# Four cross-attention key projections moved into the first batch of a recurrence, and output projections one step later

## The chip, the cores and the metric

The kernel runs on one core of a Trainium2 chip. The metric is the device time of one execution in microseconds; smaller is better. The engines are TensorE (PE; its weight loads are shown as PEld), VectorE (DVE), ScalarE (ACT), GpSimd (POOL) and SyncE (SP), whose queue starts nearly all transfers here. Each engine takes its own instructions strictly in order; semaphores tie the engines together.

## The reference

Four layers in sequence, on x (8 x 256 x 512) and a context of the same shape, all float32. L0 is an attention with an injected context. L1 is a recurrence with channel mixing, L2 a decoder block (self-attention, cross-attention, MLP), L3 a product with the context. The part that matters:

```python
# L1: for each batch, along 256 positions
a = k_l[..., :, None] * v_l[..., None, :]
out = jnp.einsum('bhs,bhst->bht', r_l, faaaa * a + s)
s_new = a + w_l[..., None] * s
...
# L2, D = 512, 16 heads of 32
ctx = merge_heads(attention(split_heads(q), split_heads(k), split_heads(v), ltor_mask))
x = hidden_states + (ctx @ w_ao + b_ao)
q = layernorm(x, ln2_s, ln2_b) @ w_q + b_q
kv = encoder_states @ w_kv + b_kv
k, v = jnp.split(kv, 2, axis=-1)
ctx = merge_heads(attention(split_heads(q), split_heads(k), split_heads(v), cross_mask))
x = x + (ctx @ w_co + b_co)
```

The keys and values of the cross-attention depend on the context input and on weights only, not on what the layers before have computed.

## The kernel before, in words

The program has three stages. `stage_l0` computes L0. `Middle` computes L1 and both attentions of L2 in one loop. `stage_mlp` does the rest. The change lies in `Middle`, whose code is in `plan`.

**The recurrence.** Its loop has 64 steps: 8 batches x 4 column tiles `ct` x 2 halves. In a step `spread` (L890, PE) writes products into the one PSUM buffer `vb`; `states` multiplies them with k (L912) and scans them (L916, two scans, DVE); POOL multiplies by r (L921); `gather` (L933, PE) sums the step before. A spread can start only when the scans of the step before have read `vb`.

**The attentions.** 16 runs of 4 steps follow: runs 0 to 7 (`a_`) are the self-attention of the batches 0 to 7, runs 8 to 15 (`c_`) the cross-attention. A step handles 4 heads of 32. In step n the loop issues the row maxima (L1121, DVE) and exponentials (L1124, ACT) of step n+1, the transpose `dt` of half of step n's probabilities (L1157, DVE, which goes through DRAM to `pt`), the scores of step n+2 (L1102, PE) with their masking (L1111 product on DVE, L1116 addition on POOL), the other half's transposes (L1146, PE), the reciprocals and divisions of step n+1 (L1132 DVE, L1134 POOL), and `values` of step n-1 (L1174, PE, copied to `cx` by ACT at L1178).

**Fillers.** All other work hangs in these loops by a `Filler`: a table from a slot number to functions. `fill.until(x)` runs all that is due up to x. In the recurrence, step n first runs `states`, then fillers up to n + 0.95, then `gather`, then fillers up to n + 0.99, then the next `spread`. In the attention a step runs its fillers up to n + 0.5 before `values` and up to n + 0.99 after it; A0 = 64 is where the attention's slots begin, and run i has its slots at A0 + 4i plus a number. So the projections of q, k and v of a run (`at_q`, `at_k`, `at_v`) lie in the steps of the run before, and its output projection (`at_out`, two halves) in the steps of the run after: half 0 at 4.6, that is after `values` of step 0 of the next run, half 1 at 5.6, after `values` of step 1. `proj` (L805) and `proj_s` (L869) are the matmuls of all of these. `at_out` adds the result to the residual tile `hv` or `csx` (L1068, DVE), `at_v` adds the bias to `av` (L1053, DVE).

**Order on the engines.** In `Middle` PE follows the program's order. On the other engines a scheduler orders by its own estimate of when an instruction's inputs are ready, except where an instruction is pinned behind the one traced before it on its engine (`pin`, that is `keep_in_program_order`). The masking, the maxima, the reciprocals, the divisions and `dt` are pinned; L1053 and L1068 are not.

**Buffers.** Weights are loaded by SP into a pool of ten halves (five pairs); a list `spans` of first and last use, sorted, decides at which slot each pair is loaded. The tags `kk` and `csx` have one buffer each, `k` has two, and the PSUM banks `mm` are three in the recurrence and eight in the attention.

Of the kernel before, what the change touches and what calls it, by code (L numbers as in the profile page):

```python
# [10 lines left out]
F32 = mybir.dt.float32  # L11
AF = mybir.ActivationFunctionType
ALU = mybir.AluOpType
# [3 lines left out]
P = 128  # L17
B, S, D = 8, 256, 512
ST = S // P
CT = D // P  # L20
# [73 lines left out]
def rows_of(halves):  # L94

    return [halves[k // 2][:, k % 2, :] for k in range(CT)]
# [513 lines left out]
class Middle:  # L610
# [62 lines left out]
    def plan(self):  # L673
        g, cp, wpool = self.g, self.cp, self.wpool
        nc, I = g.nc, g.I
# [32 lines left out]
        t_ = {}  # L708
# [91 lines left out]
        def proj(b, W, src, c2):  # L800
            pp = mm("proj")
            for j in range(2):
                o = (2 * c2 + j) * P
                for k in range(CT):
                    nc.tensor.matmul(  # L805
                        pp[:, j, :], lhsT=t_[W, b][k][:, o : o + P], rhs=src[:, k, :],
                        start=(k == 0), stop=(k == CT - 1),
                    )
            return pp
# [56 lines left out]
        def proj_s(b, W, src, st):  # L866
            pp = flat(mm("projs"))
            for k in range(CT):
                nc.tensor.matmul(  # L869
                    pp, lhsT=src[:, k, st * P : (st + 1) * P], rhs=t_[W, b][k],  # L870
                    start=(k == 0), stop=(k == CT - 1),
                )
            return pp
# [116 lines left out]
        HD, NH = 32, 4  # L990
        runs = [(pre, b) for pre in ("a_", "c_") for b in range(B)]

        def at_fetch(i):
            pre, b = runs[i]
            x = t_["axi", i] = wk.tile([P, ST, D], F32, tag="xi", name="axi", bufs=1)
            nc.sync.dma_start(out=x, in_={"a_": g.x2, "c_": g.x3, "m_": g.x4}[pre][b])
# [40 lines left out]
        def at_k(i, c2):  # L1037
            pre, b = runs[i]
            if c2 == 0:
                t_["ak", i] = wk.tile([P, CT, S], F32, tag="k", name="ak")  # L1040
            pp = proj(0, pre + "wk", t_["src", i], c2)
            for j in range(2):
                ct = 2 * c2 + j
                nc.scalar.activation(
                    t_["ak", i][:, ct, :], pp[:, j, :], AF.Identity, bias=g.pv(pre + "bk", ct)
                )

        def at_v(i, st):
            pre, b = runs[i]
            if st == 0:  # L1050
                t_["av", i] = wk.tile([P, ST, D], F32, tag="v", name="av")
            vp = proj_s(0, pre + "wv", t_["src", i], st)
            nc.vector.tensor_tensor(t_["av", i][:, st, :], vp, g.rv[pre + "bv"], ALU.add)  # L1053

        def at_residual(i):
            pre, b = runs[i]
# [7 lines left out]
        def at_out(i, st):  # L1064
            pre, b = runs[i]
            x = t_["axo", i]
            op = proj_s(0, pre + "wo", t_["cx", i], st)
            nc.vector.tensor_tensor(x[:, st, :], x[:, st, :], op, ALU.add)  # L1068

        def at_store(i):  # L1070
            pre, b = runs[i]
# [4 lines left out]
        def at_load(W, src, col):  # L1076
            t_[W, 0] = rows_of(g.weight(wpool, I[src], col, W))
# [10 lines left out]
        def at_consts2():  # L1088
            late = cp.tile([P, NMC], F32, tag="constc", name="lconstc")
            nc.scalar.dma_start(out=late[:, 0 : NRV - 2 * D], in_=I["rvec"][2 * D :].partition_broadcast(P))  # L1090
            for name, n in RVEC[2:]:
                c = RCOL[name] - 2 * D
                g.rv[name] = late[:, c : c + n]

        pin = lambda ins: self.tc.keep_in_program_order(ins)

        def scores(i, ct):
            sps = t_["sp", i, ct] = [mm("sp") for _ in range(NH)]
# [103 lines left out]
        def when(b, at):  # L1202

            if b == 0 and at in FIRST:
                return FIRST.index(at) - 30
            return 8 * (b - 1) + (at[max(0, b - B + 3)] if isinstance(at, tuple) else at)
# [3 lines left out]
        fill = self.fill = Filler()  # L1210
        for b in range(B):
            for at, fn, *args in steps + after:
                fill.put(when(b, at), lambda b=b, fn=fn, args=args: fn(b, *args))

        A0 = 8 * B
        for i in range(len(runs)):
            for at, fn, *args in (
                (-7.1, at_fetch), (-5.95, at_inputs), (-6.6, at_norm), (-5.9, at_normed), (-5.3, at_norm_T),
                (-4.8, at_q, 0), (-3.8, at_q, 1), (-2.8, at_k, 0), (-2.3, at_k, 1), (-1.3, at_v, 0), (-0.8, at_v, 1),
                (3.9, at_residual), (4.6, at_out, 0), (5.6, at_out, 1), (6.3, at_store),  # L1220
            ):
                fill.put(A0 + CT * i + at, lambda i=i, fn=fn, args=args: fn(i, *args))
        runs.append(("m_", 0))
        for at, fn in ((-6.1, at_fetch), (-5.6, at_norm), (-4.9, at_normed), (-4.3, at_norm_T)):
            fill.put(A0 + CT * (2 * B) + at, lambda fn=fn: fn(2 * B))
# [8 lines left out]
        spans = []  # L1234
# [3 lines left out]
        for pre, i, q, kv, o in (("a_", 0, "w_qkv", "w_qkv", "w_ao"), ("c_", B, "w_q", "w_kv", "w_co")):  # L1238
            c = D if q == kv else 0
            for W, lo, hi, src, col in (  # L1240
                ("wq", -4.8, -3.8, q, 0), ("wk", -2.8, -2.3, kv, c), ("wv", -1.3, -0.8, kv, c + D), ("wo", 4.6, 5.6, o, 0)
            ):
                lo, hi = A0 + CT * i + lo, A0 + CT * (i + B - 1) + hi
                spans.append((lo, hi, lambda W=pre + W, src=src, col=col: at_load(W, src, col)))
        spans.sort(key=lambda x: x[0])

        free = [-9.0, -9.0, -2.9, -0.9, 2.3]
        for lo, hi, fn in spans:
            free.sort()
            at = free.pop(0)  # L1250
# [507 lines left out]
```

## Time and profile before

| | us |
|---|---|
| three runs | 3474.51, 3485.38, 3486.36; median 3485.38 |
| profiled execution | 3492.2, its span 3490.3, mean granted clock 0.968 |
| recurrence's first spread | at 1394 |
| first transpose `dt` of the attention | at 2213 |
| last one | at 2972 |
| busy PE / DVE / ACT / POOL | 3262.3 / 2373.8 / 1606.1 / 1943.9 |
| a 512 KB load of a weight, of `enc`, of `xi`, issue to landing | 4.1 to 4.8, 4.5, 3.4 |

All stretches are counted from the start of the span. A line of instructions in order of time gives the start, the time from the first start to the last end, the engine, the line of code, the operation, the tiles, the count, and in brackets the idle time before it with what ended it. A line of waits gives who waited for whom, the total, how often, and the longest. The granted clock is TensorE's, as a share of its full speed.

### The profile page before, as it was taken

The numbers are of one execution on the slowest core, as the hardware profiler recorded it, in microseconds if no ns is written. First come the engines' busy times: TensorE is split into PE (matmuls) and PEld (weight loads), VectorE is DVE, ScalarE is ACT, GpSimd is POOL, SyncE is SP. The second block draws the span as 40 slices with busy tenths as digits, with TensorE's granted clock in tenths as the row PEclk, the third lists the DMA queues.
The fourth block names the chain that finished last, engine by engine and source line by source line (L and its number), as shares of the span: only waits on it lengthen the run. The fifth ranks groups of instructions, "written<-read, shape, count | busy, mean of one in ns | idle before, by whom it ended". The sixth has DMA issues, their size and how long they took to land. (4 is left out here: it accounts for less than half of the span.)

```text
span 3490.3 us, 68550 instructions
## 1 busy us (share of the span) xinstructions
PE 3262.3 (93%) x27008; PEld 2333.4 (67%) x27008; DVE 2373.8 (68%) x3328; ACT 1606.1 (46%) x4032; POOL 1943.9 (56%) x1870
## 2 busy tenths in 40 slices
PE   8999999999999998789999998799999998799999
PEld 6677776777777765566566665555565554699996
DVE  4666666666666663888887877565677766577771
ACT  3455555555555463233334333455656655323223
POOL 7533333333324222565565665667778888688882
PEclk9999999999999998899999999899999999899999
DMA  7666665665756533212233232244355445300002
GB/s 273 228 191 195 185 200 172 196 205 177 219 180 204 176 94 124 74 55 97 91 98 105 95 116 78 88 146 155 118 169 161 147 139 163 130 1 1 1 11 87
DMA packets 230431, 466.46 MB, mean 134 GB/s; under 512 B 19872, under 2 KB 114720, under 8 KB 226016
## 3 DMA queue, kind: packets, MB, share of 16 engines
q1 hardware_dynamic: 227648, 456.47, 40.8%
q8 instruction: 215, 3.52, 0.4%
q10 hardware_dynamic: 1808, 3.80, 0.3%
q0 software_dynamic: 656, 1.81, 0.2%
q14 instruction: 104, 0.85, 0.1%
HBM read 378.12 MB, written 83.89 MB: 132 GB/s over the span
## 5 line engine op out<-in xcount | busy, mean ns | idle before, releaser
L381 POOL TENSOR_SCALAR pe<-pe,rinv 128x512 f32<-128x512 f32 x256 | 177.8, 695 | 613.5 <-DVE rinv L380 608.3
L921 POOL TENSOR_TENSOR rs<-a,r 128x1024 f32<-128x1024 f32 x128 | 303.6, 2387 | 262.0 <-DVE a L916 259.2
L358 DVE TENSOR_REDUCE nmax<-sp 128x2 f32<-128x1024 f32 x256 | 309.0, 1218 | 185.3 <-PE sp L353 185.3
L367 ACT ACTIVATE pe<-sp,nmax 128x512 f32<-128x512 f32 x512 | 347.5, 683 | 11.4 <-ACT nmax L363 0.4
L1124 ACT ACTIVATE pe<-pe,nmax 128x256 f32<-128x256 f32 x512 | 253.3, 499 | 207.1 <-DVE nmax L1121 207.1
L393 DVE STREAM_TRANSPOSE pt<-pe 128x1024 f32<-128x1024 f32 x256 | 313.0, 1232 | 52.3 <-POOL pe L381 43.4
L422 PE MATMUL av<-pt,vr 32*64 32x256 f32 x8192 | 276.2, 397 | 38.7 <-issue 25.6
L916 DVE TENSOR_TENSOR_SCAN a<-w,vb 128x1024 f32<-128x1024 f32 x128 | 287.3, 2275 | 4.9
L422 PEld LDWEIGHTS av<-pt,vr 32*64 32x64 f32 x8192 | 213.1, 139 | 113.3 <-issue 45.7
L353 PE MATMUL sp<-k,q 64*64 64x512 f32 x2048 | 265.8, 611 | 8.2 <-ACT pe L367 8.2
L1134 POOL TENSOR_SCALAR pe<-pe,rinv 128x256 f32<-128x256 f32 x512 | 242.5, 496 | 3.1 <-DVE rinv L1132 2.3
L363 ACT ACTIVATE nmax<-nmax 128x2 f32<-128x2 f32 x256 | 51.8, 203 | 405.0 <-DVE nmax L358 404.6
L293 PEld LDWEIGHTS gp<-t,ws 128*128 128x128 f32 x1512 | 184.3, 192 | 32.0 <-issue 13.7
L1116 POOL TENSOR_TENSOR pe<-pe,lconstb 128x1024 f32<-128x1024 f32 x64 | 150.8, 2359 | 96.9 <-DVE rinv L1132 85.4
L293 PE MATMUL gp<-t,ws 128*128 128x128 f32 x1512 | 202.8, 278 | 1.9 <-POOL ws L279 1.4
L386 ACT ACTIVATE pe<-pe,rinv 128x512 f32<-128x512 f32 x256 | 182.5, 729 | 41.4 <-DVE rinv L380 41.4
L1121 DVE TENSOR_REDUCE nmax<-pe 128x4 f32<-128x1024 f32 x128 | 153.1, 1213 | 53.7 <-POOL pe L1116 53.7
L1116 POOL TENSOR_TENSOR pe<-pe,mb 128x1024 f32<-128x1024 f32 x64 | 151.1, 2361 | 66.9 <-DVE rinv L1132 65.9
L912 DVE TENSOR_TENSOR vb<-vb,k 128x1020 f32<-128x1020 f32 x128 | 157.2, 1228 | 4.4
L890 PE MATMUL vb<-v,mconstc 32*128 32x255 f32 x1024 | 99.8, 446 | 57.5 <-DVE a L916 57.5
L1438 ACT ACTIVATE h<-h,pvec 128x256 f32<-128x256 f32 x124 | 55.8, 500 | 200.7 <-DVE h L1407 163.2
L380 DVE RECIPROCAL rinv<-ssum 128x2 f32<-128x2 f32 x256 | 41.1, 161 | 147.0 <-ACT pe L367 147.0
(312 smaller groups left out, 7805.5 us busy)
## 6 DMA issues: line engine op xcount, KB each, us to landing
ws<-sqk SPq DMA_DIRECT2D x110, 512.0 KB, 5.0
wqk<-in_wqk_dram SPq DMA_DIRECT2D x71, 512.0 KB, 5.1
vr<-v SPq DMA_DIRECT2D x128, 256.0 KB, 4.8
pt<-dt SPq DMA_DIRECT2D x64, 512.0 KB, 2.6
pt<-pt SPq DMA_DIRECT2D x256, 128.0 KB, 3.1
ws<-sv SPq DMA_DIRECT2D x56, 512.0 KB, 5.0
wv<-in_wv_dram SPq DMA_DIRECT2D x36, 512.0 KB, 4.7
v<-vT SPq DMA_DIRECT2D x64, 256.0 KB, 2.6
```

Source lines behind the costliest of these rows:

```text
L293: nc.tensor.matmul(out[:, hf * P : (hf + 1) * P], lhsT=w[n](hf, k), rhs=a[n](hf, k), start=k == 0, stop=k == ST - 1,)
L353: nc.tensor.matmul(sp[a * 64 : (a + 1) * 64, h, :], lhsT=qs[b, 2 * un + a][r, ic], rhs=ks[b, 2 * un + a][r, :], start=True, stop=True,)
L358: nc.vector.tensor_reduce(nmax, sp, AX.X, ALU.max, negate=True)
L367: nc.scalar.activation(pe[:, h, :], sp[:, h, :], AF.Exp, bias=nmax[:, h : h + 1], scale=1.0 / DH ** 0.5, accum_out=ssum[:, h : h + 1],)
L386: nc.scalar.mul(pe[:, 1, :], pe[:, 1, :], rinv[:, 1:2])
L393: nc.vector.transpose(pts[b, un][:, it], pe)
L422: nc.tensor.matmul(av[r][h * DH : (h + 1) * DH], lhsT=vr[rows_, kb, h * DH : (h + 1) * DH], rhs=pt[rows_, :, h, 32 * kb : 32 * kb + 32], s ...
L916: nc.vector.tensor_tensor_scan(a.rearrange("p n l -> p (n l)"), w4.rearrange("p n l -> p (n l)"), vb[:, 4 * n2 : 4 * n2 + 4, :].rearrange( ...
L921: nc.gpsimd.tensor_tensor(rs, a, rb, ALU.mult)
L1116: pin(nc.gpsimd.tensor_tensor(pe4, pe4, b4, ALU.add))
L1124: nc.scalar.activation(pe[:, r, :], pe[:, r, :], AF.Exp, bias=nmax[:, r : r + 1], accum_out=ssum[:, r : r + 1],)
L1134: pin(nc.gpsimd.tensor_scalar(pe[:, r, :], pe[:, r, :], rinv[:, r : r + 1], 1.0, ALU.mult, ALU.mult))
```

## The change

It has three parts.

1. A key projection of the cross-attention, for batches 0 to 3 (runs 8 to 11), is computed in the first eight steps of the recurrence (`EARLY`), each from its own load of the context into `kk`, with a weight pair of its own (`c_wk0`). The result goes to `csx`, and from there to DRAM (`ck`). In the attention `at_k` loads it from DRAM into the tile `ak` in place of the projection. Runs 12 to 15 stay as they were.
2. The additions L1053 (`at_v`) and L1068 (`at_out`) are pinned.
3. The first half of the output projection goes from slot 4.6 to 5.2: from the end of step 0 to the middle of step 1, before `values`. The time at which its weights are expected moves with it.

```diff
+        pin = lambda ins: self.tc.keep_in_program_order(ins)
...
+            if pre == "c_" and b in ck:
+                if c2 == 0:
+                    nc.sync.dma_start(out=t_["ak", i], in_=ck[b])
+                return
...
+        EARLY = {0: (-0.3, 0.6, 1.6), 1: (1.7, 2.6, 3.2), 2: (3.25, 3.8, 4.6), 3: (4.7, 7.3, 7.7)}
+        ck = {}
+
+        def ck_load(b):
+            t_["enc", b] = wk.tile([P, CT, S], F32, tag="kk", name="enc", bufs=1)
+            nc.sync.dma_start(out=t_["enc", b], in_=I["ctxT"][b].rearrange("(k p) s -> p k s", p=P))
+
+        def ck_part(b, c2):
+            if c2 == 0:
+                t_["ck", b] = new("csx", 1)
+            pp = proj(0, "c_wk0", t_["enc", b], c2)
+            for j in range(2):
+                ct = 2 * c2 + j
+                nc.scalar.activation(t_["ck", b][:, ct, :], pp[:, j, :], AF.Identity, bias=g.pv("c_bk", ct))
+            if c2 == 1:
+                ck[b] = g.dram([P, CT, S], f"ck{b}")
+                nc.sync.dma_start(out=ck[b], in_=t_.pop(("ck", b)))
...
-            nc.vector.tensor_tensor(t_["av", i][:, st, :], vp, g.rv[pre + "bv"], ALU.add)
+            pin(nc.vector.tensor_tensor(t_["av", i][:, st, :], vp, g.rv[pre + "bv"], ALU.add))
...
-            nc.vector.tensor_tensor(x[:, st, :], x[:, st, :], op, ALU.add)
+            pin(nc.vector.tensor_tensor(x[:, st, :], x[:, st, :], op, ALU.add))
...
+        for b, (lo, *at) in EARLY.items():
+            fill.put(lo, lambda b=b: ck_load(b))
+            for c2 in range(2):
+                fill.put(at[c2], lambda b=b, c2=c2: ck_part(b, c2))
...
-                (3.9, at_residual), (4.6, at_out, 0), (5.6, at_out, 1), (6.3, at_store),
+                (3.9, at_residual), (5.2, at_out, 0), (5.6, at_out, 1), (6.3, at_store),
...
-                ("wq", -4.8, -3.8, q, 0), ("wk", -2.8, -2.3, kv, c), ("wv", -1.3, -0.8, kv, c + D), ("wo", 4.6, 5.6, o, 0)
+                ("wq", -4.8, -3.8, q, 0), ("wk", -2.8, -2.3, kv, c), ("wv", -1.3, -0.8, kv, c + D), ("wo", 5.2, 5.6, o, 0)
...
+        spans.append((0.55, 7.75, lambda: at_load("c_wk0", "w_kv", 0)))
```

More of the change, by code (lines that the diff above doesn't have):

```diff
@@ L1093, in at_consts2 @@
                 g.rv[name] = late[:, c : c + n]
-        pin = lambda ins: self.tc.keep_in_program_order(ins)
         def scores(i, ct):
```

## The prediction

> **What bounds the kernel now.** I read the page's busy shares first, then stretches of the span, the waits of the attention, and last the single instructions of each engine in order of time.
>
> ```profile
> PE 3262.3 (93%) x27008; PEld 2333.4 (67%) x27008; DVE 2373.8 (68%) x3328; ACT 1606.1 (46%) x4032; POOL 1943.9 (56%) x1870
> ```
>
> TensorE looks like the limit. By stretch (us of window, then busy PE, PEld, DVE, ACT, POOL, the clock, DMA share, GB/s) it is not so simple: 1399 to 1447 is the beginning of the recurrence, 2720 to 2765 is attention run 10.
>
> ```profile
> 1399.00:1447.00 48.00, 35.86 (x246) 24.20 (x245) 44.85 (x49) 5.11 (x10) 30.15 (x14) 0.82 0.11 34
> 2346.00:2391.00 45.00, 45.00 (x256) 27.32 (x255) 25.86 (x37) 23.60 (x77) 27.60 (x32) 1.00 0.47 153
> 2720.40:2764.90 44.50, 41.95 (x266) 26.71 (x265) 31.84 (x50) 27.53 (x89) 36.79 (x43) 1.00 0.47 151
> 2809.40:2855.40 46.00, 43.23 (x265) 27.58 (x264) 31.87 (x51) 27.88 (x91) 36.77 (x44) 0.96 0.44 144
> ```
>
> Early in the recurrence VectorE is the full engine (44.85 of 48) and PE has holes, at a low clock. Runs 0 to 3 of the attention still carry the recurrence's leftover matmuls: PE is 45.00 of 45 there. From run 4 on, PE is idle some 2.5 us a run. The waits of 2446 to 2945 name it (total, times, longest):
>
> ```profile
> DVE csx L1068 <- PE projs L869: 39.9, 12, 5.6
> PE projs L869 <- ACT cx L1178: 25.7, 10, 2.6
> ```
>
> The first output projection of a run waits for the last context tile, and VectorE waits for that projection before the next row maxima. What these waits cost is read from the cycle that carries a step. VectorE's transpose `dt` comes once a step, the mask addition on GpSimd follows:
>
> ```profile
> 2709.11 1.25 DVE L1157 STREAM_TRANSPOSE dt<-pe 128x1024 f32<-128x1024 f32 x1 [0.60 <-POOL pe L1134]
> 2710.28 1.25 DVE L1111 TENSOR_TENSOR pe<-sp,mk 128x512 f32<-128x512 f32 x2
> ...
> 2720.39 1.25 DVE L1157 STREAM_TRANSPOSE dt<-pe 128x1024 f32<-128x1024 f32 x1 [0.61 <-POOL pe L1134]
> ...
> 2728.85 0.69 DVE L1068 TENSOR_TENSOR csx<-csx,projs 128x512 f32<-128x512 f32 x1 [2.56 <-PE projs L869]
> 2729.46 2.34 DVE L1121 TENSOR_REDUCE nmax<-pe 128x4 f32<-128x1024 f32 x2
> 2731.71 1.24 DVE L1157 STREAM_TRANSPOSE dt<-pe 128x1024 f32<-128x1024 f32 x1
> ```
>
> `dt` waits for GpSimd's last division of the step before; GpSimd's next step waits for the mask product behind `dt`. GpSimd's step is 2 x 2.36 + 2 x 1.85 = 8.42 us (L1116, L1134), `dt` and the mask product 2 x 1.17, hand-overs some 0.2: 10.95. Measured starts of `dt` in run 9 are 2675.9, 2687.2, 2698.1, 2709.1, 2720.4: steps of 11.33, 10.93, 10.99, 11.28. So this GpSimd-VectorE cycle, at 10.92 to 10.95 us, sets the step; the wait of 2.56 us at L1068 cost 0.39 of it, GpSimd's residual additions 0.33. PE only has to keep up. Runs 4 to 13 last 47.21, 46.14, 44.45, 45.88, 45.92, 44.53, 44.53, 44.52, 45.92, 45.92 us (455.02); run 14 lasts 43.70. The longer ones have a lower clock (0.93 and 0.96 above), and PE limits some of their steps (12.28, 12.23 us).
>
> **Part 1: four key projections go into batch 0's recurrence.** Added there: four times two halves of 16 PE records. One half measures 3.55 us start to start at full clock, so 8 x 3.55 = 28.4 us of PE work, 16 evictions on ScalarE (0.42 each, ScalarE is 5.11 busy of 48), and on SP's queue one more weight pair, four loads of `enc`, four stores of `ck`. The cover is PE's idle time:
>
> ```profile
> 1434.61 2.08 PE L890 MATMUL vb<-v,mconstc 32*128 32x255 f32 x16 [6.28 <-DVE a L916]
> 1436.62 5.03 PE L805 MATMUL proj<-x_maa_k,Wk 128*128 128x256 f32 x16
> ...
> 1482.68 2.08 PE L890 MATMUL vb<-v,mconstc 32*128 32x255 f32 x16 [7.71 <-DVE a L916]
> ```
>
> Gaps of 4.32, 1.54, 6.28 and 7.71 us before spreads 1, 2, 4 and 8 make 19.85. After a gap PE runs slow: the spread takes 2.08 instead of 1.07, Wk 5.03 instead of 3.55. With the gaps filled that excess goes too; over 1404 to 1447 I count some 6 us of it. So 28.4 - 25.9 = 2.5 us at least.
>
> By place: batch 0's first half fits into the 4.32. The second half stands before the gather and the `mp` matmuls of step 1, delaying the next vb copy 0.5 us. Batch 1's first half lies between Wg and hp: delay 1.9 in all. In step 3 the new order has 7.1 us of PE before the gather, and they cannot run through: batch 2's `enc` shares one buffer with batch 1's and is issued only when that batch's last half is done (about 1431.9 by my count); a 512 KB load lands after 3.4 us at the quickest of the like rows (xi 3.4, enc 4.5), so PE stands some 3.9 us, and `mp` and spread 4 end near 1442 instead of 1436.7: 5.7. One more half in step 4 makes 7.2 to 7.6; steps 5 and 6 are limited by PE (13.00 of 13, 14.97 of 15 busy), so nothing is won back there; batch 3's 7.1 us fit the 7.71, and the warm spread returns 1.0. Sum **+6.6**. Bounds: 2.5 (all cover used) and 21.3 (nothing usable but the last gap, 28.4 - 7.1). I take 6.6 because each place was walked through.
>
> The gate: idle 6.28 us was followed by matmuls at 5.03/3.55 of their warm time, but idle 2.59 us was too (run 4's next two projection records: 2.08 against 1.13), in 4 of 10 cases. The Trainium skill, "TensorE: Matmul & The Clock Gate", Part 1, says the clock drops after an idle window of about 3.4 us. By that rule gaps of 2 us would never be slow, and the ordinary runs below would gain 5 us where I put 2; it also speaks against taking matmuls out of the attention, since that opens longer gaps.
>
> SP: what queues behind the new waits (Wr's second half, Wg of batch 1) is needed from step 6.3 and 8.5 on, 50 us later: nothing.
>
> **Part 2: what leaves the attention.** Keys of runs 8 to 11 were projected in the steps of runs 7 to 10: 7.1 us of PE each, and 4 evictions each. But those steps follow the GpSimd cycle. With 7.1 us of slack PE no longer limits any, and the L1068 wait goes: 10.94 + 10.94 + 10.99 + 11.27 = 44.14 a run, 176.6 against 45.88 + 45.92 + 44.53 + 44.53 = 180.9: **-4.3**. The `ck` loads (512 KB) are queued one run early, since their buffer is free then; the transposes' own transfers (2.6 and 3.1 us) have a whole step: nothing, and at most 3 us each if they collide.
>
> **Part 3: first output projection to the next step, additions pinned.** In the order of instructions only L1068 moves: before, the first addition stood ahead of the row maxima of the next step; now both stand together, one step's end later. The `av` additions (L1053) stay where they were, except one near the recurrence's end that no longer sits between two scans (0.66 us, **-0.6**).
>
> Step 0 of a run loses its 0.39. Step 1, however, now has on PE: transposes 0.95, projection 3.5, keys 3.55, values 1.0, projection 3.5, keys 3.55, scores 1.1. Its transposes wait for GpSimd's division, 4.2 us before `dt`. So the second projection ends 8.3 us after `dt`; add hand-over 0.2, one addition 0.65, two maxima 2.35: the next `dt` at 11.6 instead of 10.94, **+0.7**. PE also idles in step 0, in two pieces (1.7 and 2.1 us) where it had one of 2.6. Run: 10.95 + 11.65 + 10.99 + 11.27 = 44.86 if warm. The six ordinary runs (4, 5, 6, 11, 12, 13) took 274.2; six times 44.86 is 269.2, so -5.0 if none is slow, and +1.0 if four lose 1.5 as four did. I take the middle, **-2.0**: the gaps are shorter, but there are two. Run 14, at 43.70: **+0.7**. Runs 0 to 3 are full of PE work whose amount stays: 0 (bounds -6, the idle between 2212 and 2335 that nothing here touches, and +3 x 2.9 if step 1 turns slow).
>
> Sum: 6.6 - 4.3 - 2.0 + 0.7 - 0.6 = +0.4 us. The profiled execution took 3492.2 (span 3490.3); the median shown is 3485.4, 0.2% lower. Its term: **3486**.
>
> **Rivals.**
> 1. PE is the bound after all: 28.4 us of keys and 25.7 us of context waits come off, the early part costs 6.6: -47, 3438. For it: 93% busy, 41.95 of 44.50. Against it: steps of 10.92 to 10.94 whatever PE did in them, and run 14, with PE at 40 of 44, no quicker than those.
> 2. The clock stays up and the cover is used fully: early +2.5, ordinary runs -5.0, keys -4.3, rest as above: -7; with half the idle of runs 0 to 3 (6 us) also gone, 3472.
> 3. Slower: step 1's overload. PE enters it after an idle stretch, runs slow for its first matmuls (2.2 us more, as in the 12.28 and 12.23 us steps together), and the second projection holds VectorE's maxima. Place: L1068 ahead of L1121. Price 2.9 us in ten runs (1 to 6, 11 to 14), some 29, less the 8 us which the slow runs already pay, less 4.3, plus 6.6: +23, 3509. It decides when a step 1 exceeds 13 us in most runs.
>
> **How the numbers follow.** 0.5% is 17 us, about what a measurement tells from no change. Forecast (within 3478 to 3496) 0.54; rival 2 0.18, most of it above 3468; rival 1, whole or by half, 0.10; rival 3, or an early part nearer its upper bound, 0.18. Faster by over 0.5%: 0.10 and a fifth of rival 2, 0.14. Slower: 0.16. Same: 0.70. The range leaves out rival 1 and the far end of rival 3: 3464 to 3510.
>
> **What would show it.** Right: matmuls of `c_wk0` in the gaps of 1400 to 1447, the clock there above 0.82, PE waiting some 4 us for `enc` once, step 8 reached some 7 us later; no wait of PE for `cx`; `dt` steps of 10.9 in step 0, 11.6 in step 1, runs 7 to 10 at 44.1. Wrong: runs under 43.7 us (then GpSimd's cycle was not the bound), step 1 over 13, or `dt` late for `ak`.

## The result, and the profile after

The changed kernel took 3491.93 us (median of 12 runs, 3483.38 to 3498.4); the kernel before, on the same chip, took 3479.64 us (3474.51 to 3487.13). The ratio is 1.0032, 95% interval 1.0022 to 1.0042: some 11 us slower, which is inside the 0.5% that the prediction called no change. The forecast of 3486 us is 6 us low and the range held the time, but several of its terms were wrong and offset each other. The 6 us flatter the forecast: it was the median of three runs (3485.38) with a change of +0.4, that median lies 5.7 us over the one of all twelve, and the change itself was some 11 us. The profiled execution took 3497.65 us, its span is 3495.9 us.

The busy shares of the changed kernel, from the page's first part:

```profile
PE 3283.5 (94%) x27008; PEld 2343.8 (67%) x27008; DVE 2369.9 (68%) x3328; ACT 1607.3 (46%) x4032; POOL 1940.0 (55%) x1870
```

The number of matmuls is the same (x27008), but PE is busy 21 us longer: some of them took more time. Two stretches of the changed kernel (window, its length, busy PE, PEld, DVE, ACT, POOL, clock, DMA share, GB/s) answer to those shown of before, the recurrence's beginning and attention run 10:

```profile
1399.00:1447.00 48.00, 41.16 (x261) 30.39 (x260) 35.94 (x40) 7.72 (x18) 25.33 (x11) 0.93 0.23 77
2721.50:2767.80 46.30, 39.38 (x233) 22.90 (x233) 31.83 (x51) 26.29 (x85) 36.70 (x43) 0.91 0.45 143
```

In the recurrence PE's holes are mostly filled and its clock is higher (0.93, 0.82 before), but VectorE, which was full (44.85 of 48), now stands a quarter of the time: 35.94. The bound engine was made to wait. In run 10 there are 33 matmul records fewer, and yet the run takes 46.30 us for 44.50, at clock 0.91 for 1.00.

The recurrence first. PE, the sync engine's queue and VectorE of the changed kernel in order of time (start, duration, engine, line, operation, in brackets the idle time before it and what ended it):

```profile
1428.01 3.72 PE L805 MATMUL proj<-enc,c_wk 128*128 128x256 f32 x16
...
1436.19 6.49 PE L805 MATMUL proj<-enc,c_wk 128*128 128x256 f32 x16 [4.46 <-DVE a L916]
...
1431.76 0.37 SPq L1060 DMA_DIRECT2D enc<-in_ctxT_dram  x1
...
1444.78 0.88 DVE L765 SCALAR_TENSOR_TENSOR x_maa_v<-mp,pvec,sx 128x256 f32<-128x256 f32 x2 [8.70 <-PE mp L762]
```

Batch 2's `enc` is issued when batch 1's last half ends (1428.01 + 3.72), PE stands 4.46 us for it, and the 16 matmuls behind the stand take 6.49 us where the same 16 took 3.72 just before. The profile puts the stand down to VectorE's scan `a` (L916); that it is the load is shown by an experiment below. VectorE stands 8.70 us for the shift's `mp`. The steps of the recurrence, read from the starts of VectorE's `vb` copy (L909), are 10.07, 12.69, 17.52, 12.10 us for steps 1 to 4, where before had 8.65, 10.79, 10.11, 10.44.

Then the attention. In runs 7, 9 and 10 the last step takes 13.93, 13.74 and 13.56 us. The changed kernel in run 7:

```profile
2617.00 1.25 DVE L1180 STREAM_TRANSPOSE dt<-pe 128x1024 f32<-128x1024 f32 x1 [0.59 <-POOL pe L1157]
...
2620.68 2.16 DVE L68 TENSOR_SCALAR axn<-axi,ln_mv,ln_rstd 128x512 f32<-128x512 f32 x2
2622.76 0.67 DVE L1078 TENSOR_TENSOR av<-projs,lconstc 128x512 f32<-128x512 f32 x1
2626.63 1.29 DVE L58 BATCH_NORM_STATS2 ln_stats<-axi 128x6 f32<-128x512 f32 x2 [3.20 <-DMA axi<-xa]
2627.83 0.16 DVE L59 BATCH_NORM_AGGREGATE ln_mv<-ln_stats 128x2 f32<-128x6 f32 x1
2627.91 0.84 DVE L1034 TENSOR_SCALAR aq<-proj,pvec 128x256 f32<-128x256 f32 x2
2628.67 2.33 DVE L1144 TENSOR_REDUCE nmax<-pe 128x4 f32<-128x1024 f32 x2
2630.93 1.23 DVE L1180 STREAM_TRANSPOSE dt<-pe 128x1024 f32<-128x1024 f32 x1
...
2622.86 0.34 SPq L998 DMA_DIRECT2D axi<-xa  x1
...
2628.81 5.83 PE L805 MATMUL proj<-ln,c_wq 128*128 128x256 f32 x16 [4.13 <-DVE aq L1034]
```

The row statistics of a later run's input (L58) now stand ahead of the queries' eviction `aq`, the maxima and `dt`. Their input's load can be issued only when `axn` has read the one buffer that it shares (2622.86), so VectorE stands 3.20 us with everything queued behind it: `dt` is 13.93 us behind the last. PE waits 4.13 us for `aq` and then runs slow (5.83 for 16 matmuls that take 3.62). Before, the same instruction stood in the next step, behind the reciprocals, and waited for nothing; that step of the kernel before begins with the `dt` of the first line:

```profile
2629.94 1.25 DVE L1157 STREAM_TRANSPOSE dt<-pe 128x1024 f32<-128x1024 f32 x1 [0.60 <-POOL pe L1134]
...
2633.53 0.16 DVE L1132 RECIPROCAL rinv<-ssum 128x4 f32<-128x4 f32 x1
2633.61 1.25 DVE L58 BATCH_NORM_STATS2 ln_stats<-axi 128x6 f32<-128x512 f32 x2
```

No line of the diff touches this instruction, and it is not pinned: the scheduler placed it.

Of the waits shown of before, PE's for the context tile (25.7 us in 2446 to 2945) has no line any more in 2451 to 2949, and VectorE's for the first projection is halved (total, times, longest):

```profile
DVE csx L1093 <- PE projs L869: 19.2, 6, 4.8
```

So the waits that the change aimed at went. They were worth little, and the two above came.

### The profile page after: what moved, and what is told of

Its sections match the earlier page's. It is cut to its first block, busy times and chain, and to the rows that moved or that the text cites. A ratio compares the mean times of both kernels' runs of the same rounds, so it can differ in the third digit from the quotient of the medians.

```text
span 3495.9 us, 68561 instructions
## 1 busy us (share of the span) xinstructions
PE 3283.5 (94%) x27008; PEld 2343.8 (67%) x27008; DVE 2369.9 (68%) x3328; ACT 1607.3 (46%) x4032; POOL 1940.0 (55%) x1870
## 5 line engine op out<-in xcount | busy, mean ns | idle before, releaser
L367 ACT ACTIVATE pe<-sp,nmax 128x512 f32<-128x512 f32 x512 | 347.0, 683 | 11.4 <-ACT nmax L363 0.4
L916 DVE TENSOR_TENSOR_SCAN a<-w,vb 128x1024 f32<-128x1024 f32 x128 | 287.1, 2275 | 5.1
```

The source lines that it names most:

```text
L367: nc.scalar.activation(pe[:, h, :], sp[:, h, :], AF.Exp, bias=nmax[:, h : h + 1], scale=1.0 / DH ** 0.5, accum_out=ssum[:, h : h + 1],)
L916: nc.vector.tensor_tensor_scan(a.rearrange("p n l -> p (n l)"), w4.rearrange("p n l -> p (n l)"), vb[:, 4 * n2 : 4 * n2 + 4, :].rearrange( ...
```

## The experiments

One number must come first: how far a ratio can be read. The stretch ahead of the recurrence, where the change moves nothing on PE or VectorE, ended between 1384.9 and 1395.2 us in the profiled executions, with no relation to the kernel. Each experiment is therefore read twice: by its ratio to the kernel before, and by the stretch of its trace from the recurrence's first `vb` copy to the last `dt` of the attention, all in us:

| kernel | ratio (95% interval) | recurrence to first `dt` | runs 0-3 | 4-6 | 7-10 | 11-13 | 14 | whole stretch |
|---|---|---|---|---|---|---|---|---|
| before | 1 | 817.5 | 233.5 | 137.8 | 180.9 | 136.4 | 43.7 | 1576.7 |
| before again (e13) | 1.0007 (0.9998-1.0017) | 814.3 | 235.9 | 134.9 | 177.8 | 133.4 | 43.6 | 1566.9 |
| changed | 1.0032 (1.0022-1.0042) | 827.5 | 229.4 | 133.3 | 183.6 | 136.0 | 45.2 | 1582.0 |
| changed again (e12) | 1.0043 (1.0028-1.0057) | 827.6 | 229.7 | 136.2 | 182.9 | 134.7 | 44.1 | 1582.2 |
| e1: parts 2+3 | 0.9981 (0.9968-0.9994) | 813.8 | 228.2 | 134.8 | 180.8 | 136.3 | 44.1 | 1565.0 |
| e2: part 1 | 1.0044 (1.0031-1.0057) | 827.8 | 229.7 | 134.6 | 188.6 | 134.9 | 43.6 | 1586.1 |
| e3b: statistics held | 0.9997 (0.9987-1.0007) | 827.5 | 227.7 | 136.2 | 176.0 | 136.1 | 45.9 | 1576.4 |
| e4: two `enc` | 1.0004 (0.9990-1.0018) | 820.1 | 228.9 | 137.0 | 182.9 | 134.7 | 44.1 | 1574.7 |
| e5: both mends | 0.9982 (0.9972-0.9992) | 820.4 | 227.6 | 136.2 | 176.3 | 136.1 | 46.0 | 1569.5 |
| e6: part 2 | 0.9990 (0.9980-1.0000) | 816.6 | 231.1 | 133.5 | 177.8 | 136.3 | 43.7 | 1565.9 |
| e7: part 3 | 1.0004 (0.9993-1.0016) | 814.3 | 228.9 | 133.6 | 180.9 | 136.3 | 44.1 | 1565.0 |
| e9: parts 2+3, statistics held | 0.9968 (0.9956-0.9980) | 813.7 | 226.2 | 132.9 | 177.6 | 132.5 | 46.8 | 1556.6 |
| e10: the same, less one | 0.9996 (0.9983-1.0009) | 813.8 | 225.3 | 133.8 | 177.5 | 134.1 | 45.9 | 1557.4 |
| e11: e10, projection at 4.6 | 1.0016 (1.0004-1.0028) | 813.9 | 233.7 | 135.1 | 181.9 | 136.9 | 43.6 | 1572.0 |

The first four experiments ran on one chip; e5, e6 and e9 on another; e7, e10 and e11 on a third; e12 and e13 on a fourth. e1 and e7 differ by the place of one addition, and have the same stretch (1565.0), but ratios of 0.9981 and 1.0004. So ratios of different groups compare to about 0.2% (8 us), whatever their intervals; within a group they are better. The stretch of kernels nearly alike repeats within 1 us (changed 1582.0 and 1582.2, e1 and e7, e9 and e10), with one exception: the kernel before itself. (The two stretches of the changed kernel agree in sum, while their columns 4-6 and 11-13 differ by 2.9 and 1.3.)

**e1: without the early keys.** Of the changed kernel, the table of early keys is empty and their weights are not loaded:

```diff
-        EARLY = {0: (-0.3, 0.6, 1.6), 1: (1.7, 2.6, 3.2), 2: (3.25, 3.8, 4.6), 3: (4.7, 7.3, 7.7)}
+        EARLY = {}
...
-        spans.append((0.55, 7.75, lambda: at_load("c_wk0", "w_kv", 0)))
```

> This kernel has parts 2 and 3 alone: the additions of av and of the output projection in program order and the first output projection at 5.2 for 4.6; no early keys, so the keys of runs 8 to 11 are projected in the runs as before. Theory (the changed kernel lost 10 to 12 us in the early part and 7.8 us in a new wait of DVE for axi in step 3 of runs 7, 9 and 10, and won some 6 us back in the ordinary runs): the stall of 8.70 us for mp in the recurrence and the wait of 3.20 us for axi are both gone, since both come from the early part and from what its removal of the later keys does to the scheduler's order; runs 4 to 6 take 133 to 134 us together, as in the changed kernel, against 137.8 before; the time is 3 to 9 us under the kernel before. Rival (the moved projection gains nothing, and the profiled execution of before merely had slow steps in runs 4 and 5 that its median does not have): within 3 us of the kernel before.

Measured: 0.9981, 6.6 us under the kernel before. The stall in the recurrence is gone (step 3 takes 10.11) and so is the wait for `axi`. Runs 4 to 6 take 134.8, a little over what was expected, because run 4 has one slow step (12.08). The theory's two losses both come with part 1.

**e2: the early keys alone.** The kernel before with the early table, its loads, halves and stores, and the runs' key loads:

```diff
+            if pre == "c_" and b in ck:
+                if c2 == 0:
+                    nc.sync.dma_start(out=t_["ak", i], in_=ck[b])
+                return
...
+        for b, (lo, *at) in EARLY.items():
+            fill.put(lo, lambda b=b: ck_load(b))
+            for c2 in range(2):
+                fill.put(at[c2], lambda b=b, c2=c2: ck_part(b, c2))
...
+        spans.append((0.55, 7.75, lambda: at_load("c_wk0", "w_kv", 0)))
```

> This kernel is the one before with part 1 alone: the early keys through DRAM, without the additions in program order and with the first output projection at 4.6. Theory: the early part costs 10 to 12 us, the wait for axi 2.5 us in three or four runs, 7.5 to 10 together, and the keys that are left out of runs 8 to 11 give 2 to 5 us back: 13 to 18 us over the kernel before, and so slower than the changed kernel. Rival (the prediction's own terms: early +6.6, keys -4.3): 2 us over the kernel before.

Measured: 1.0044, 15.3 us over the kernel before, as the theory had it and not the 2 us of the prediction's terms. The recurrence takes 827.8, the same as in the changed kernel, and now four runs, 7 to 10, have a last step of 13.5 to 13.8 us. So the displaced statistics belong to the keys' removal, not to the additions held in order.

**e3b: the statistics back in their place.** In the changed kernel, the statistics of the cross-attention inputs are held in program order in step 0, and the load of `axi` is issued 1.2 steps earlier:

```diff
-            t_["ast", i] = ln_stats(g, sm, t_["axi", i])
+            t_["ast", i] = ln_stats(g, sm, t_["axi", i], pin if i >= B else lambda ins: ins)
...
+                at = {at_fetch: -8.3, at_norm: -7.6}.get(fn, at) if i >= B else at
                 fill.put(A0 + CT * i + at, lambda i=i, fn=fn, args=args: fn(i, *args))
```

> The changed kernel with the row statistics of runs 4 to 11's inputs held in step 0, behind the reciprocals, where the kernel before had them, and the load of axi 1.2 steps earlier; the application axn then comes in step 1. Theory: DVE no longer waits for axi ahead of aq, PE has no stand of 4.13 us with cold matmuls behind it, step 3 of runs 7, 9 and 10 takes 11.2 us and not 13.6 to 13.9: 6 to 8 us under the changed kernel, 4 to 6 over the kernel before. Rival (the wait only takes the place of another one in that step, such as PE's for aq, or the statistics put their 2.6 us into step 0 instead): 0 to 2 us under the changed kernel.

(The edit holds for the inputs of runs 8 to 15, whose statistics stand two runs ahead, in runs 6 to 13; the "runs 4 to 11" of this and two later expectations is a slip. It also holds the statistics of the stage after the attention.) Measured: 0.9997. Runs 7 to 10 fall from 183.6 and 182.9 to 176.0, 44.0 each. The same place in run 7 of this kernel:

```profile
2616.34 1.25 DVE L1180 STREAM_TRANSPOSE dt<-pe 128x1024 f32<-128x1024 f32 x1 [0.59 <-POOL pe L1157]
...
2620.02 0.66 DVE L1078 TENSOR_TENSOR av<-projs,lconstc 128x512 f32<-128x512 f32 x1
2620.60 0.86 DVE L1034 TENSOR_SCALAR aq<-proj,pvec 128x256 f32<-128x256 f32 x2
2621.38 1.21 DVE L1144 TENSOR_REDUCE nmax<-pe 128x4 f32<-128x1024 f32 x1
2625.44 1.22 DVE L1144 TENSOR_REDUCE nmax<-pe 128x4 f32<-128x1024 f32 x1 [2.85 <-POOL pe L1139]
2627.25 1.25 DVE L1180 STREAM_TRANSPOSE dt<-pe 128x1024 f32<-128x1024 f32 x1 [0.60 <-POOL pe L1157]
```

`aq` comes 4.26 us behind `dt`, not 10.91, VectorE waits for GpSimd alone, and the step is 10.91: the GpSimd-VectorE cycle of the prediction, with nothing on top. In the stretch the mend brings 5.7 us: 7.2 in runs 7 to 10, less some in others. The ratios say 12 and more, across groups; only the 5.7 to 7.2 are accounted for by the trace.

**e4: two buffers for the early `enc`.** The loads of batches 1 to 3 are issued earlier, and nothing else in PE's or VectorE's work is altered:

```diff
-        EARLY = {0: (-0.3, 0.6, 1.6), 1: (1.7, 2.6, 3.2), 2: (3.25, 3.8, 4.6), 3: (4.7, 7.3, 7.7)}
+        EARLY = {0: (-0.3, 0.6, 1.6), 1: (0.58, 2.6, 3.2), 2: (1.7, 3.8, 4.6), 3: (3.25, 7.3, 7.7)}
...
-            t_["enc", b] = wk.tile([P, CT, S], F32, tag="kk", name="enc", bufs=1)
+            t_["enc", b] = wk.tile([P, CT, S], F32, tag=("kk", "g")[b % 2], name="enc", bufs=1 + b % 2)
```

> The changed kernel with two buffers for the early enc in turn, and the loads of batches 1, 2 and 3 issued 1.1 to 1.5 steps earlier; DVE's order is the same, and so is the work of PE. Theory: of the loss in the recurrence the larger part is PE's stand of 4.46 us for the late load of batch 2 and the slow clock behind it (16 matmuls 6.49 us, not 3.62), so step 3 takes 10.5 to 12 us and not 17.5, and the time is 5 to 7 us under the changed kernel. Rival (the early work's 28 us of PE are themselves what the recurrence can't hide, and the landing of the load does not matter): 0 to 2 us under the changed kernel, with steps 3 to 5 longer than in the kernel before by as much as now.

Measured: 1.0004. PE of this kernel in step 3, and VectorE's next product:

```profile
1426.83 7.17 PE L805 MATMUL proj<-enc,c_wk 128*128 128x256 f32 x32
1433.93 1.07 PE L933 MATMUL yp<-rs,mconstc 128*32 128x256 f32 x16
...
1436.10 0.88 DVE L765 SCALAR_TENSOR_TENSOR x_maa_v<-mp,pvec,sx 128x256 f32<-128x256 f32 x2 [1.20 <-PE mp L762]
```

Both halves run through in 7.17 us at full clock, VectorE waits 1.20 us instead of 8.70, and step 3 takes 10.03 instead of 17.52. The scan `a` is where it was, so the stand was the load's, whatever the bracket said. That makes 7.5 us of the early loss in step 3, and 6.9 by step 8, as step 4 is 0.5 longer. Steps 0 to 7 together still take 94.12 against 89.6 to 89.8 without early keys, +4.4, and this stays in e5 (93.96). The rival is refuted for the larger part; for the smaller one it holds.

**e5: both mends**, the edits of e3b and e4 together, repeated here by their core:

```diff
+        EARLY = {0: (-0.3, 0.6, 1.6), 1: (0.58, 2.6, 3.2), 2: (1.7, 3.8, 4.6), 3: (3.25, 7.3, 7.7)}
...
+                at = {at_fetch: -8.3, at_norm: -7.6}.get(fn, at) if i >= B else at
```

> Both mends at once: the statistics of runs 4 to 11's inputs held in step 0 and two buffers with earlier loads for the early enc. Theory: the two losses lie in different places (recurrence step 3; attention runs 7, 9 and 10) and add up: 7 to 8 us from the one and 7 to 11 from the other, 15 to 19 us under the changed kernel and 6 to 10 under the kernel before (0.997 to 0.998). Rival (what is saved early is lost again where PE is behind in runs 0 to 3): within 3 us of either mended kernel, so about the time of the kernel before.

**e6: the additions in program order alone** (e1 with the first projection and its weights at 4.6).

```diff
-                (3.9, at_residual), (5.2, at_out, 0), (5.6, at_out, 1), (6.3, at_store),
+                (3.9, at_residual), (4.6, at_out, 0), (5.6, at_out, 1), (6.3, at_store),
...
-                ("wq", -4.8, -3.8, q, 0), ("wk", -2.8, -2.3, kv, c), ("wv", -1.3, -0.8, kv, c + D), ("wo", 5.2, 5.6, o, 0)
+                ("wq", -4.8, -3.8, q, 0), ("wk", -2.8, -2.3, kv, c), ("wv", -1.3, -0.8, kv, c + D), ("wo", 4.6, 5.6, o, 0)
```

> Part 2 alone: the additions of av and of the output projection in program order, the first output projection still at 4.6, no early keys. In the order of instructions this moves a single one, an addition of av at the end of the recurrence. Theory: the additions in program order do nothing by themselves, and the 7 us that parts 2 and 3 won together are the moved projection's: the time is within 2 us of the kernel before, the first DVE transposition of each attention step lies 11.3 us behind the last one of the run before in undisturbed runs, as in the kernel before. Rival (the order of the addition at the end of the recurrence is what won): 5 to 8 us under the kernel before. Its profile is also a second look at the order of the kernel before: if the steps over 11.5 us in runs 4, 5, 7, 8, 12 and 13 lie elsewhere here, they are chance and not that order's.

**e9: e3b's edit in e1**, so no early keys:

```diff
+        EARLY = {}
...
+                at = {at_fetch: -8.3, at_norm: -7.6}.get(fn, at) if i >= B else at
```

> Parts 2 and 3 without the early keys, with the statistics of runs 4 to 11's inputs held in step 0 and their load 1.2 steps earlier. It tells what the early keys are worth once both their waits are mended: this kernel against the one with both mends. Theory: keys left out of runs 8 to 11 give at most 0.5 us per run (44.0 us against 44.5) and a slow step of 1.5 us here and there, some 2 to 5 us, and the early part still costs 4 us by recurrence step 8, so the two kernels lie within 3 us of each other; this one is 5 to 9 us under the kernel before. Rival (the early keys gain as PE is relieved in the cross-attention): the kernel with both mends is over 4 us faster than this one.

Measured together on one chip: e5 0.9982, e6 0.9990, e9 0.9968. The two mends add up: the stretch of e5 is 12.6 us under the changed kernel's, where e3b and e4 had 5.7 and 7.4. By the ratios it is 6.3 us under the kernel before. But the kernel without early keys is 4.5 us faster still by the medians of this group, and 12.8 in the stretch of the profiles; the theory for e9 had put them within 3. So the early keys lose even when both their waits are mended. They lose 4.2 us up to step 8 of the recurrence. Up to the first `dt` it is 6.7 (820.4 against 813.7), but behind step 8 e5 loses 3.2 in three steps (26, 33, 34) that also differ by 3.3 between the two profiles of the kernel before, as is shown under e13, so how much of this is the keys' own stays open. In the attention the early keys win 1.3 in runs 7 to 10 and lose elsewhere. One place is run 6: there GpSimd, whose cycle is the bound, stands 2.11 us in e5 (2.38 in e3b) for the load of the residual `csx`, and step 3 takes 12.90 us against 10.92 in e9, which has no such wait. In e5 that load was issued right behind the first `ck` load and landed after 10.6 us, in e9, without a `ck` load, after 8.4. Another is run 11, the first one for whose next run keys are projected again. PE of e5:

```profile
2753.74 2.39 PE L1125 MATMUL sp<-ak,aq 32*128 32x256 f32 x16 [0.99 <-DVE pe L1134]
2757.29 2.27 PE L1169 MATMUL tp<-ident,pe 128*128 128x128 f32 x8 [1.17 <-POOL pe L1157]
2759.35 5.55 PE L869 MATMUL projs<-c_wo,cx 128*128 128x512 f32 x8
```

and e9 at the same place:

```profile
2738.98 2.06 PE L1125 MATMUL sp<-ak,aq 32*128 32x256 f32 x16
2742.21 1.91 PE L1169 MATMUL tp<-ident,pe 128*128 128x128 f32 x8 [1.17 <-POOL pe L1157]
2743.96 3.60 PE L869 MATMUL projs<-c_wo,cx 128*128 128x512 f32 x8
```

With the keys gone from the run before, PE has two holes (0.99 and 1.17 us) where e9 has one, and its eight wide matmuls take 5.55 us for 3.60: step 1 of run 11 is 13.11 us against 11.26. In windows around these lines the granted clock is 0.64 in e5 (2759.3 to 2764.8) and 1.00 in e9 (2744.0 to 2747.4). e3b, the other kernel with early keys and held statistics, has the same two holes (0.99 and 1.16 us) and takes 5.61 us for the same matmuls. Here the relief of PE was paid back in clock; that the second hole comes of the missing keys fits the order of the work, and was not tried by itself.

e6 moves one instruction against the kernel before, and its ratio of 0.9990 touches 1. Its profile is a second look at nearly the same order: step 0 is 11.3 us in runs 4 to 12, and the slow steps of runs 4, 5, 7 and 8 are not there (44.40, 44.69, 44.42, 44.46 for 47.21, 46.14, 45.88, 45.92), while those of 12 and 13 are.

**e7, e10, e11: what the moved projection is worth.** e7 is the kernel before with part 3 alone; e10 is e9 with the statistics of the stage after the attention not held; e11 is e10 with e6's edit. The edits of e7 and of e10:

```diff
-                (3.9, at_residual), (4.6, at_out, 0), (5.6, at_out, 1), (6.3, at_store),
+                (3.9, at_residual), (5.2, at_out, 0), (5.6, at_out, 1), (6.3, at_store),
...
-                ("wq", -4.8, -3.8, q, 0), ("wk", -2.8, -2.3, kv, c), ("wv", -1.3, -0.8, kv, c + D), ("wo", 4.6, 5.6, o, 0)
+                ("wq", -4.8, -3.8, q, 0), ("wk", -2.8, -2.3, kv, c), ("wv", -1.3, -0.8, kv, c + D), ("wo", 5.2, 5.6, o, 0)
```

```diff
-            t_["ast", i] = ln_stats(g, sm, t_["axi", i], pin if i >= B else lambda ins: ins)
+            t_["ast", i] = ln_stats(g, sm, t_["axi", i], pin if B <= i < 2 * B else lambda ins: ins)
```

> Part 3 alone: the kernel before with the first output projection at 5.2 for 4.6, no additions in program order, no early keys. It differs from parts 2 and 3 together by the place of one addition at the end of the recurrence. Theory: the move by itself is worth 3 to 7 us (parts 2 and 3 were 7 us under the kernel before, part 2 alone 4 us, both with some 4 us of uncertainty). Rival: the move is worth nothing, and this is within 2 us of the kernel before.

> Parts 2 and 3 without the early keys, the statistics of the inputs of the cross-attention runs 8 to 15 held in step 0 two runs ahead, as in the kernel that was 10 us under before, but the statistics of the stage after the attention left to the order they had (there DVE had waited 2.32 us for them in step 2 of run 14, a step of 13.27 us). Theory: run 14 takes 44.1 and not 46.8 us, the rest as in that kernel: 11 to 14 us under the kernel before (0.996 to 0.997). Rival: the wait comes back after the last step: 8 to 11 us under.

> The kernel beside it with the first output projection back at 4.6: it tells what the moved projection is worth once nothing else differs. Theory: step 0 of each run takes 11.3 instead of 10.9 us and step 2 10.95 instead of 11.0 to 11.4, so the move gains nothing that can be told apart, and the two kernels lie within 3 us. Rival (the wait for the first projection ahead of the maxima is what costs, 0.4 us in 14 runs and a slow step now and then): this kernel is 4 to 8 us over the one beside it.

Measured: 1.0004, 0.9996 and 1.0016. e10 misses its expectation: DVE's wait in run 14 is gone, but run 14 still takes 45.9 us (its step 1 is 12.67) and run 13 has a slow step of 12.36. Its stretch is that of e9, 9.5 us under the better execution of before, while the ratios of the two lie 0.3% apart; what can be said is that this version lies between the time of the kernel before and 0.3% under it.

The moved projection alone (e7) can't be told from the kernel before by its ratio. Beside e11, e10 is 7.8 us faster by the medians and 14.7 in the stretch, the number of the rival and not the theory's 3 us, but there something else differs, too. VectorE of e11 in step 0 of run 9:

```profile
2662.56 1.25 DVE L1180 STREAM_TRANSPOSE dt<-pe 128x1024 f32<-128x1024 f32 x1 [0.60 <-POOL pe L1157]
...
2670.57 1.95 DVE L68 TENSOR_SCALAR axn<-axi,ln_mv,ln_rstd 128x512 f32<-128x512 f32 x2 [1.88 <-ACT ln_rstd L61]
2672.44 0.67 DVE L1093 TENSOR_TENSOR hv<-hv,projs 128x512 f32<-128x512 f32 x1
2673.03 2.33 DVE L1144 TENSOR_REDUCE nmax<-pe 128x4 f32<-128x1024 f32 x2
2675.29 1.23 DVE L1180 STREAM_TRANSPOSE dt<-pe 128x1024 f32<-128x1024 f32 x1
```

With the first addition held in step 0, the scheduler put `axn` before it; it waits 1.88 us for ScalarE's `ln_rstd`, and step 0 becomes 12.73 us in runs 6 to 13. In e10 `axn` stands in step 1, beside the additions. So the pair shows how much a step of VectorE is worth that holds one wait too many (1.8 us a run), and not the pure worth of the projection's move.

**e12 and e13: both kernels again, unaltered.**

> The changed kernel once more, unaltered, on the chip that also runs the kernel before once more: what of the step lengths is the instruction stream's own, and what is chance of one execution. Kernels alike up to the recurrence began it anywhere from 1384.9 to 1395.2 us. Theory: recurrence step 3 takes 17.5 us again, step 3 of runs 7, 9 and 10 takes 13.6 to 13.9 us again, the stretch from the recurrence's first step to the last attention step is 1580 to 1583 us again, and only the start differs. Rival: the slow steps lie elsewhere, and the stretch differs by 5 us or more.

> The kernel before, unaltered. Theory (the slow steps are the stream's own): 12.2 us in step 0 of runs 4, 5, 8 and 13 again and 1576 to 1578 us from the recurrence's first step to the last attention step, so the changed kernel is 4 to 6 us over it in that stretch. Rival (the profiled execution of before was a slow one; the order that differs by one addition took 1566 us): 1564 to 1570 us, and the changed kernel 12 to 17 us over it. Its ratio to the kernel before is that of a kernel to itself, 1.000, and tells how far a ratio can be trusted.

Measured: 1.0043 and 1.0007. The changed kernel repeats: recurrence step 3 takes 17.49 us, step 3 of runs 7, 9 and 10 takes 13.42, 13.53 and 13.66, the stretch 1582.2. Its slow steps of other runs wander (12 to 14 in the first profile; 5, 6 and 12 in this one). The kernel before does not repeat: its stretch is 1566.9 us, and after run 4 it has no slow step at all. Run 10 of this execution:

```profile
2704.30:2748.70 44.40, 41.68 (x266) 26.43 (x265) 31.82 (x50) 27.50 (x89) 36.69 (x43) 1.00 0.48 153
```

So the rival was right: the profiled execution of before, on which the prediction's sum was made, was longer in this stretch, by 10 us. Against e13 the changed kernel is 15.2 us longer in the stretch, which is what the ratios say (11 and 15 us).

The granted clock in the kept traces says what differed between the two. In all profiles it is either full or half. The half-clock stretches last 3.41 us or whole multiples of it (the one cut off by the program's end apart), and in each execution all of them start on one grid of 3.41 us, to within 3 ns. Here is one, at the slow step of run 12 in the first profile of before; the clock is the third number from the end:

```profile
2815.00:2818.20 3.20, 1.46 (x10) 0.69 (x14) 0.64 (x2) 1.68 (x3) 3.20 (x4) 1.00 0.45 128
2818.30:2821.70 3.40, 3.40 (x22) 2.61 (x19) 3.40 (x4) 1.94 (x8) 2.02 (x5) 0.50 0.02 5
2821.80:2825.10 3.30, 3.30 (x19) 2.63 (x22) 2.71 (x7) 2.96 (x12) 1.77 (x1) 1.00 0.38 159
```

The work lies differently on this grid in each execution. An undisturbed run of 44.47 us is 13 widths of the grid and 0.10 us, so the starts of the runs move slowly along it. Take runs 6 to 13 of before, e13 and e6, which have the same order there: the 18 runs whose first `dt` starts 0.65 to 1.24 us behind a line of the grid are undisturbed, and the six that start 1.29 to 1.39 or 2.79 to 2.93 us behind one have a half-clock stretch and last 45.88 to 45.93 us. In e1 and e7 the eight that start at 2.29 to 2.56 are undisturbed, and the eight at 2.59 to 2.68 or 0.94 to 1.10 last 45.62 to 46.21. So which runs are slow went with their place on the grid, without an exception in these 40 runs; no run set the place on purpose. The recurrence depends on it, too: in steps 26, 33 and 34 the first profile of before took 3.3 us more than e13, with 6.8 us at half clock for 3.4 where step 26 begins and 3.4 us for none in step 33.

## Why the prediction was right or wrong

The time was right within 6 us, and this was in good part luck: of the change, +0.4 was forecast and some 11 measured, and the sum came no further off only because a gain that no term held set off the terms that were too small. The reading that the GpSimd-VectorE cycle sets the step was right (about 10.9 us in the undisturbed steps of every kernel), and so PE's relief could not bring the 47 us of rival 1. Rival 2, the cover fully used, did not come: every version with early keys took longer from the recurrence's start to the first `dt` than any without. The terms, by the mean of two profiles of each kernel:

- **Early part, put at +6.6, measured +11.6** up to the first `dt` (827.55 against 815.9; +13.3 against e13 alone), and this includes the `av` addition's -0.6. The mechanism was the one foretold, place included: the single buffer, the issue at 1431.76 (1431.9 by the prediction's count), a stand of 4.46 us (3.9). The step that failed is "`mp` and spread 4 end near 1442": step 3 was to bring the delay from 1.9 to 5.7, 3.8 us more, and brought 7.4. The matmuls behind the stand were counted at full speed and took 2.9 us more, though the prediction itself had shown that matmuls after such a gap run slow; and PE went on 4.43 us after the load's issue, where 3.4 had been put. Steps 1 and 2 were undersized too, +1.4 and +1.9 us for 0.5 and 1.4; step 4 (+1.7) and the 0.9 won back in step 7 were as foretold. e4 shows the stand, with the slow matmuls, as 7.5. Behind step 8, for which the prediction put nothing, steps 12, 13 and 30 won 1.5 back and steps 26, 33 and 34 took 3.2 us more than in e13, the same three that the clock's grid made longer in the first profile of before.
- **Keys of runs 8 to 11, put at -4.3, measured +3.9** (183.3 against 179.3; +5.4 against e13 alone). Two steps failed. One is "176.6 against 45.88 + 45.92 + 44.53 + 44.53": the two long runs belonged to that execution and not to the order, as e13 (44.42 to 44.48) and e6 (44.42 to 44.47) show, and what the keys' removal could win was 0.4 us a run, as runs 8 (44.0) and e3b show. The other is "In the order of instructions only L1068 moves": three runs' statistics moved ahead of `aq`, with no visible tie to the key projections whose removal moved them. It cost 2.5 us in each of three runs. The `ck` loads were put at nothing, and the changed kernel shows no wait for them; in e3b and e5 the load behind one of them cost 2 us in run 6.
- **Ordinary runs, put at -2.0, measured -1.1** (runs 4 to 6 and 11 to 13 together, 270.1 against 271.2; +1.8 against e13 alone). Step 0 lost its 0.4, as said. Step 1 at 11.6 (the prediction's own addends make 11.5) was not seen in runs 4 to 6 of the first profile (10.91), where step 2 grew to 11.4 instead; step 1 was 11.7 to 12.6 in the slow steps of runs 12 to 14. Rival 3's point (step 1 over 13 us in most runs) was not reached: of its ten runs only 1, 2 and 3 had such a step (18.1, 17.0, 13.6), and there step 0 was 3 to 8 us shorter.
- **Run 14, put at +0.7, measured +1.0.**
- **Runs 0 to 3, put at 0 within -6 and +8.7, measured -5.2** (229.5 against 234.7). This gain was not in the sum, though it lies within the bounds, and it hid most of the stall. The kernels with the moved projection have 225.3 to 229.7 here and those without it 229.7 to 235.9, so it goes with the move; e2, with the keys and without the move, has 229.7, so a share of the keys is not excluded. How it comes about was not tried.

The rest, ahead of the recurrence and behind the last `dt`, is +1 us and was not followed up. The differences add to 11.2 us, the difference of the mean spans (3491.75 and 3480.55).

Of the signs that were to show it right, five came (`c_wk0` in the gaps, the clock at 0.93 for 0.82, the one wait for `enc`, no wait for `cx`, step 0 at 10.9) and three did not: step 8 was 11.3 us later and not 7, step 1 was not 11.6, and of runs 7 to 10 only run 8 took 44.

The rule cited in the prediction, from the Trainium skill's page "TensorE: Matmul & The Clock Gate", Part 1, that the clock drops after about 3.4 us of idleness, agrees with the stand of 4.46 us (matmuls at 6.49 for 3.62): the clock fell 3.3 us into it. In the stand of 4.13 us (matmuls at 5.83) it fell after 1.6 us. Nor does the rule cover e5's run 11, where two holes of 0.99 and 1.17 us were followed by eight matmuls at 5.55 for 3.60, while e9 after a hole of 1.17 us ran at full clock. The same part says that the window runs freely, so that the turning point depends on where in it the matmuls fall; the grid of 3.41 us under e13 agrees with this, and with it that slow steps wander between executions of one kernel (before: runs 4, 5, 7, 8, 12 and 13, then run 4 alone).

## What to carry to other kernels

When a scheduler orders the instructions, taking work away can move an instruction that has nothing to do with it: compare the whole order, engine by engine, and look for a moved instruction that now waits for a late transfer ahead of the chain that sets the end. A gap is cover only if the inputs are there when it opens; a wait in it costs twice, once itself and once in the slow matmuls behind it. And before a sum is made against one profiled execution, ask which of its long steps another execution would not have, and look whether they stand at half clock: a gain that consists in removing them is no gain.

## What the runs showed of the hardware that was not expected

- One and the same kernel had 10 us more or less in 1570 between two executions: 9 us in runs 4 to 13, 3.3 in the recurrence, less 2.4 in runs 0 to 3. Steps of 11.7 to 12.3 us lay in six attention runs in the one and in none after run 4 in the other. They come in neighbouring runs (4 and 5, 7 and 8, 12 and 13), at a lower granted clock (0.96 in run 12 of the first profile of before, 1.00 in run 10), and went with the run's place on the clock's grid of 3.41 us: a slow run of 45.9 us is 13 widths and 1.5 us, and so moves the next one to another place.
- Two kernels that differ by one addition repeat each other's slow steps exactly: step 1 of runs 7 and 12 takes 12.55 us in e1 and in e7, step 1 of runs 8 and 13 12.05 and 12.00, then 12.06 and 11.98. In both the recurrence began within 0.02 us of a line of the grid. So a slow step is not mere noise, and does not belong to the instruction stream alone either.
- A stretch of 3.41 us in which TensorE was partly busy can be followed by half clock: in the stand of 4.13 us it had worked 1.4 of the 3.3 us up to the fall.
- The time at which the recurrence began, after 1385 us of work that was not altered, spread over 10 us (1384.9 to 1395.2). This alone is 0.3% of the kernel.
